# First layer of a four-layer kernel: strips stored in blocks of 16 columns, values formed once per strip, one bias tile for both query halves

## The chip, the cores and the metric

The kernel runs on one core of one Trainium2 chip. The metric is the device time of one execution in microseconds; the median of several runs is compared. A core has five engines with instruction streams of their own, which meet through semaphores: TensorE (PE, whose weight loads are listed apart as PEld), VectorE (DVE), ScalarE (ACT), GpSimd (POOL) and SyncE (SP, which here only starts DMAs). TensorE writes its results to PSUM, and DVE or ACT move them from there to SBUF.

## The reference

The program is a stack of four residual layers on images of shape (2, 128, 128, 128). Only the first is touched: a group norm, and then overlapping window attention. Each window of 16 x 16 pixels asks; its keys and values are the 32 x 32 pixels around it, so neighbouring windows share keys and values. The part of the reference that matters, with WS = 16, HS = 8, NH = 4 heads of 32 channels:

```python
xp = jnp.pad(x, ((0, 0), (HS, HS), (HS, HS), (0, 0)), mode='reflect')
w = xp[:, rows][:, :, :, cols]                      # windows of 32 x 32, step 16
center = w[:, HS:HS + WS, HS:HS + WS].reshape(-1, WS * WS, C)
kv = w.reshape(-1, WSH * WSH, C)
q = (center @ Wq.T + bq) ...                        # 256 queries of a window
k = (kv @ Wk.T + bk) ...; v = (kv @ Wv.T + bv) ...  # 1024 keys and values
attn = jnp.einsum('bhqd,bhkd->bhqk', q, k) * scale
attn = attn + bias[:, start:start + WS * WS, :][None]   # by relative position
out = jnp.einsum('bhqk,bhkd->bhqd', jax.nn.softmax(attn), v)
out = out @ Wp.T + bp
...
x = x + layer0(group_norm(x))
```

The other three layers (a Fourier layer with a feed-forward part, a convolution by FFT, a selective scan) follow one after the other. All arithmetic is in float32.

## The kernel before

`layer0` walks over 2 images x 8 rows x 8 windows, 128 windows. A window has 256 queries, in two halves of 128 (`qt` 0 and 1); one half of one window is a unit, and the loop over `u` has one slot for each unit. Each image is normalised by statistics that are taken beforehand; the normalised, transposed image is kept in **strips** of 16 rows and 144 columns (128 and 8 reflected ones at each side), `xs_[b, k]` of shape [128 channels, 16, 144]. A window uses the strips `wh` and `wh + 1`. Three strips are held at a time.

`strip_load` (L219) loads half a strip, `strip_group` (L230) turns four image rows with four transposes and writes them, scaled and shifted, to the strip with one DVE instruction (L238). `strip_sides` (L242) reflects the sides on POOL. `keys` (L247) forms the keys of a strip in six pieces of 384 columns into `kc`. This work for the strip after next, and the statistics of the next image, are cut into pieces that `background` (L470) puts at the ends of the slots.

For each window, `pixels` (L287) copies its two 16 x 32 patches together on POOL (L294), `queries` (L299) makes `qT` with two matmuls of 128 columns (L305) and one DVE instruction (L311), and `values` (L317) makes the 1024 values in two groups of four matmuls (L323). ACT evicts the first group (L328), DVE the second (L330).

For each unit, `scores` (L332) multiplies queries and keys, 4 heads x 512 keys at a time; `biased` (L348) adds the relative bias and finds the largest score in one DVE instruction for each head (L358); `exponentials` (L364) takes the least of the negated maxima (L368) and runs four ACT instructions over 1024 elements (L370); `turn` (L375) transposes 512 probabilities (L385) and copies them out, on DVE (L388) for the pieces 0, 2, 4 and on ACT (L390) for the pieces 1, 3, 5, 6, 7; `outputs` (L392) multiplies probabilities and values (L401).

For each window, `reciprocals` (L406), `spread` (L419), `weighted` (L431), `project` (L440) and `measure` (L460) divide by the sums, project, add the residual, store, and take statistics for the next layer. `spread` turns the reciprocals with two matmuls against the identity (L423).

The relative bias lies in one tile of 2 halves x 4 heads x 1024, loaded by 32 DMAs on ACT's queue (L179). The PSUM buffers set much of the order: `tps` for transposes has two, `misc` only one, and every piece of keys, queries, values, projection, measurement and background goes through that one. `in_order` (L114) fixes each engine's order as written:

```python
                if first:
                    project(m - 1)
                if second and edge(m + 1):
                    values(m + 1, 0)
                if live:
                    turn(u, 4)
...
                if second:
                    spread(m)
                if ahead:
                    exponentials(u + 1)
                if second and edge(m + 1):
                    values(m + 1, 1)
                if live:
                    outputs(u)
```

`first` is the slot of a window's first half, `second` that of its second half. Between windows of one image `edge` holds; at the change of image the strips and the window's queries and values are made at once instead.

Of the kernel before, what the change touches and what calls it, by code (L numbers as in the profile page):

```python
# [134 lines left out]
def layer0(tc, cs, ins, x, x1, stats1):  # L135
# [3 lines left out]


    nc = tc.nc
    NH, HD, WS, HS = 4, 32, 16, 8
    HP = HW + 2 * HS
    NW = HW // WS
    qscale = HD ** -0.5
    with ExitStack() as ctx:
# [19 lines left out]

        bias = w.tile([P, 2, NH, 1024], F32, name="relbias")
        tab = ins["table_rev"]
        for qt in range(2):
            for h in range(NH):  # L170
                for r in range(4):
                    ry = HS + 4 * qt + r
                    src = bass.AP(
                        tab.tensor,
                        tab.offset + h * tab.shape[1] + 736 - 31 - 47 * ry,
                        [[1, 32], [47, 32], [1, 32]],
                    )
                    p0 = 96 - 32 * r
                    nc.scalar.dma_start(  # L179
                        bias[p0 : p0 + 32, qt, h, :].rearrange("p (a b) -> p a b", b=32), src  # L180
                    )

# [12 lines left out]
        stats, affine = {}, {}  # L195
        xs_, kc = {}, {}

# [21 lines left out]
        def strip_load(b, k, half):  # L219
            r0 = 16 * k - 8 + 8 * half  # L220
            flip = r0 < 0 or r0 >= HW
            if flip:
                r0 = 1 if r0 < 0 else HW - 9
            xl = two.tile([P, 8, C], F32, name=f"xs_{b}_{k}_{half}", tag="xl")
            nc.sync.dma_start(xl, x[b, r0 : r0 + 8].rearrange("r w c -> w r c"))
            if half == 0:
                xs_[b, k] = three.tile([P, WS, HP], F32, name=f"xp_{b}_{k}", tag="xp")
            xs_[b, k, half] = (xl, flip)

        def strip_group(b, k, half, g, ps, tag):  # L230
            xl, flip = xs_[b, k, half]
            sc, sh = affine[b]
            tps = ps.tile([P, 4, P], F32, name=f"xq_{b}_{k}_{half}_{g}", tag=tag)
            for j in range(4):
                r = 4 * g + j
                nc.tensor.transpose(tps[:, j, :], xl[:, 7 - r if flip else r, :], cs.ident)
            r = 8 * half + 4 * g
            nc.vector.tensor_scalar(  # L238
                xs_[b, k][:, r : r + 4, HS : HS + HW], tps, sc, sh, ALU.mult, ALU.add
            )  # L240

        def strip_sides(b, k):  # L242
            xp = xs_[b, k]
            nc.gpsimd.tensor_copy(xp[:, :, 0:HS], xp[:, :, 2 * HS : HS : -1])
            nc.gpsimd.tensor_copy(xp[:, :, HS + HW : HP], xp[:, :, HP - 10 : HP - 18 : -1])

        def keys(b, k, j):  # L247
            if j == 0:
                kc[b, k] = three.tile([P, WS, HP], F32, name=f"kc_{b}_{k}", tag="kc")
            cols = slice(384 * j, 384 * j + 384)  # L250
            kps = ps_m.tile([P, 512], F32, name=f"kps_{b}_{k}_{j}", tag="misc")
            nc.tensor.matmul(
                kps[:, 0:384], wt["k"], xs_[b, k].rearrange("p a b -> p (a b)")[:, cols],
                start=True, stop=True,
            )
            nc.vector.tensor_scalar(
                kc[b, k].rearrange("p a b -> p (a b)")[:, cols], kps[:, 0:384],
                bcol["k"], None, ALU.add,
            )

        def strip_now(b, k):
            for half in range(2):
                strip_load(b, k, half)
                for g in range(2):
                    strip_group(b, k, half, g, ps_t, "tps")
            strip_sides(b, k)
            for j in range(6):
                keys(b, k, j)

        wins = [(b, wh, ww) for b in range(NB) for wh in range(NW) for ww in range(NW)]  # L270
# [15 lines left out]

        def pixels(m):  # L287

            b, wh, ww = wins[m]
            c0 = ww * WS  # L290
            v = held.setdefault(m, {})
            xw = one.tile([P, 2, 512], F32, name=f"xw_{m}", tag="xw")
            for g in range(2):
                nc.gpsimd.tensor_copy(  # L294
                    xw[:, g].rearrange("p (a b) -> p a b", b=32), xs_[b, wh + g][:, :, c0 : c0 + 32]
                )
            v["xw"] = xw

        def queries(m):  # L299
            b, wh, ww = wins[m]  # L300
            c0 = ww * WS
            v = held.setdefault(m, {})
            qps = ps_m.tile([P, 512], F32, name=f"qps_{m}", tag="misc")
            for g in range(2):
                nc.tensor.matmul(  # L305
                    qps[:, P * g : P * g + P], wt["q"],
                    xs_[b, wh + g][:, 8 - 8 * g : 16 - 8 * g, c0 + HS : c0 + HS + WS],
                    start=True, stop=True,
                )
            qT = two.tile([P, 256], F32, name=f"qT_{m}", tag="qT")  # L310
# [5 lines left out]

        def values(m, g):  # L317
            v = held[m]
            if g == 0:
                v["v"] = two.tile([P, 8, P], F32, name=f"v_{m}", tag="v")  # L320
            vps = ps_m.tile([P, 512], F32, name=f"vps_{m}_{g}", tag="misc")
            for j in range(4):
                nc.tensor.matmul(  # L323
                    vps[:, j * P : (j + 1) * P], v["xw"][:, g, j * P : (j + 1) * P], wt["v"],
                    start=True, stop=True,
                )
            if g == 0:
                nc.scalar.copy(v["v"][:, 0:4, :], vps)  # L328
            else:
                nc.vector.tensor_copy(v["v"][:, 4:8, :], vps)  # L330

        def scores(u, g):  # L332

            m, qt = divmod(u, 2)
            b, wh, ww = wins[m]
            c0 = ww * WS
            v = held[m]
            v["sps", qt, g] = []
            for h in range(NH):
                hp = slice(HD * h, HD * h + HD)  # L340
                sps = ps_s.tile([P, 512], F32, name=f"sps_{u}_{g}_{h}", tag=f"sps{h}")
                nc.tensor.matmul(  # L342
                    sps, v["qT"][hp, qt * P : (qt + 1) * P], kc[b, wh + g][hp, :, c0 : c0 + 32],
                    start=True, stop=True,
# [3 lines left out]
        def biased(u, g, h):  # L348
# [3 lines left out]
            if g == 0 and h == 0:  # L352
                v["s", qt] = two.tile([P, NH, 1024], F32, name=f"s_{u}", tag="s")
                v["nm", qt] = two.tile([P, 3, NH], F32, name=f"nm_{u}", tag="nm")
                if qt == 0:
                    v["sums"] = two.tile([P, 2, NH], F32, name=f"sums_{m}", tag="sums")
            cols = slice(512 * g, 512 * g + 512)
            nc.vector.tensor_tensor_reduce(  # L358
                v["s", qt][:, h, cols], v["sps", qt, g][h], bias[:, qt, h, cols],
                op0=ALU.add, op1=ALU.min, scale=-1.0, scalar=3.0e38,  # L360
# [31 lines left out]
        def outputs(u):  # L392
            m, qt = divmod(u, 2)
            v = held[m]
            if qt == 0:
                v["ops"] = ps_o.tile([P, 256], F32, name=f"ops_{m}", tag="ops")
            pT = v["pT", qt]
            for j in range(8):
                for h in range(NH):
                    hp = slice(HD * h, HD * h + HD)  # L400
                    nc.tensor.matmul(  # L401
                        v["ops"][hp, qt * P : (qt + 1) * P], v["v"][:, j, hp], pT[:, h, j, :],
                        start=(j == 0), stop=(j == 7),
# [15 lines left out]
        def spread(m):  # L419
            v = held[m]  # L420
            rps = ps_m.tile([P, 512], F32, name=f"rps_{m}", tag="misc")
            for qt in range(2):
                nc.tensor.matmul(  # L423
                    rps[:, qt * P : (qt + 1) * P], v["recx"][:, qt, :], cs.ident,
                    start=True, stop=True,
                )
# [43 lines left out]
        def background(u):  # L470
# [13 lines left out]
            if b + 1 < NB:  # L484
# [9 lines left out]
                else:  # L494
# [14 lines left out]
                    if 12 <= t <= 14:  # L509
                        keys(b + 1, 0, t - 12)  # L510

        slots = 2 * len(wins)
        with in_order(tc):
# [5 lines left out]
            strip_now(0, 0)  # L519
            strip_now(0, 1)  # L520
            residual(0)
            pixels(0)
            queries(0)
            values(0, 0)
            values(0, 1)
            for u in range(-1, slots + 3):
# [3 lines left out]
                if qt == 1 and ahead and (m + 1) % (NW * NW) == 0 and m >= 0:  # L530

                    b = wins[m + 1][0]
                    for j in (3, 4, 5):
                        keys(b, 0, j)
                    strip_now(b, 1)
                    pixels(m + 1)
                    queries(m + 1)
                    values(m + 1, 0)
                    values(m + 1, 1)
                edge = lambda n: n < len(wins) and n % (NW * NW) != 0  # L540
# [13 lines left out]
                if first:  # L554
                    project(m - 1)
                if second and edge(m + 1):
                    values(m + 1, 0)
                if live:
# [8 lines left out]
                if qt == 0 and 0 <= m < len(wins):  # L567
                    if m + 1 < len(wins):
                        residual(m + 1)
                    if edge(m + 1):  # L570
                        pixels(m + 1)
                        queries(m + 1)
                if second:
                    spread(m)
                if ahead:
                    exponentials(u + 1)
                if second and edge(m + 1):
                    values(m + 1, 1)
                if live:
                    outputs(u)  # L580
                if first:
                    measure(m - 1)
# [1289 lines left out]
```

## Time and profile before

| what | value |
|---|---|
| time, median of 3 runs | 18506.04 us (18495.7 to 18506.94) |
| the profiled execution: its time, its span | 18497.56 us, 18495.8 us |
| first exponential of the first layer (L370) | 119.53 us |
| last reciprocal of the first layer (L410) | 3408.1 us |
| layer 0, strip transposes evicted (L238) | 809 ns each, 72 |
| values on PE (L323) | 2048 records, 304.2 us busy |
| values evicted on ACT (L328), on DVE (L330) | 585 ns and 692 ns each, 128 of each |
| pixel copies on POOL (L294) | 612 ns each, 256 |
| query matmuls (L305) | 512 records, 79.4 us busy |
| reciprocals turned on PE (L423) | 512 records, 78.2 us busy |
| biased scores on DVE (L358) | 683 ns each, 2048 |

A matmul of two float32 operands has two records in the trace, a transpose one. Records on PE overlap, so that busy time is smaller than the number of records times their mean duration. In the timeline a row has the start, the duration, the engine, the line, the operation with what it writes and reads, how many were merged, and in brackets how long the engine stood idle before it and who released it. The whole first layer is about 3,419 us of the span; the remaining layers take the rest.

### The profile page before, as it was taken

The page shows a single profiled execution, that of the slowest core. Times are in us where ns is not written, and L with a number is a line of the kernel's source. Part 1 is how long each engine was busy: PE and PEld are TensorE (multiplying, and loading weights), DVE is VectorE, ACT ScalarE, POOL GpSimd, SP SyncE. Part 2 cuts the span into 40 slices and gives each one's busy share as a digit, 9 for nine tenths or more (in the row PEclk, how much of TensorE's full clock was granted, in tenths as well). Part 3 has the DMA queues.
Part 4 walks back from the last instruction along what each step waited for, and adds up shares of the span by engine and source line. Part 5 has one row for each costly group of instructions (what it writes and reads, how often), then busy time and mean ns, then how long its engine had stood idle before and what let it go on. Part 6 is the DMA issues. An engine that isn't in the chain of part 4 may idle for free. (4 is left out here: it accounts for less than half of the span.)

```text
span 18495.8 us, 280256 instructions
## 1 busy us (share of the span) xinstructions
PE 14497.6 (78%) x98938; PEld 8455.1 (46%) x98938; DVE 15999.1 (87%) x20731; ACT 14932.9 (81%) x30141; POOL 11956.1 (65%) x6710
## 2 busy tenths in 40 slices
PE   7888888887567777777777777777777777777778
PEld 5665666674223344444444444444444444444445
DVE  6666666335888899999999999999999999999996
ACT  4665666333445799999999999999999999999984
POOL 0000000011000399999999999999999999999981
PEclk9999999889779899999999998999999989999999
DMA  2000000121114544444444454544444444455546
GB/s 49 23 23 22 16 16 16 55 72 55 49 48 147 174 119 119 118 126 126 127 114 119 120 128 126 126 118 116 120 126 127 126 122 115 116 122 128 132 129 191
DMA packets 1228553, 1861.32 MB, mean 101 GB/s; under 512 B 120781, under 2 KB 587469, under 8 KB 1224846
## 3 DMA queue, kind: packets, MB, share of 16 engines
q1 hardware_dynamic: 1157374, 1817.40, 37.2%
q10 hardware_dynamic: 69776, 26.00, 0.6%
q8 instruction: 785, 12.86, 0.3%
q14 instruction: 618, 5.06, 0.1%
HBM read 1398.48 MB, written 444.60 MB: 100 GB/s over the span
## 5 line engine op out<-in xcount | busy, mean ns | idle before, releaser
L1599 DVE TENSOR_TENSOR_SCAN hs<-da,states,ups 128x512 f32<-128x512 f32 x8192 | 9920.7, 1262 | 248.9 <-PE ups L1591 235.9
L1617 POOL TENSOR_TENSOR hs<-hs,cb 128x2048 f32<-128x2048 f32 x2048 | 9406.4, 4593 | 310.1 <-POOL but L1554 185.2
L1591 PE MATMUL ups<-ident,but 128*128 128x128 f32 x32768 | 5576.7, 301 | 2578.9 <-DVE hs L1599 1718.8
L1591 PEld LDWEIGHTS ups<-ident,but 128*128 128x128 f32 x32768 | 3873.7, 151 | 6179.9 <-DVE hs L1599 3526.1
L1559 ACT ACTIVATE but<-du,bt 128x256 f32<-128x256 f32 x12800 | 5328.7, 497 | 4.7 <-DVE du L1440 4.2
L1535 ACT ACTIVATE da<-db,na 128x512 f32<-128x512 f32 x8192 | 5224.1, 710 | 19.1 <-DMA db<-dd 17.8
L1573 PE MATMUL yps<-hs,sel 128*32 128x512 f32 x16384 | 2495.2, 685 | 60.7 <-POOL hs L1617 48.2
L1554 POOL TENSOR_TENSOR but<-du,bt 128x256 f32<-128x256 f32 x3584 | 2148.8, 620 | 15.2 <-DVE du L1440 15.2
L282 POOL TENSOR_TENSOR xres<-xres,rowb 128x256 f32<-128x256 f32 x128 | 93.2, 728 | 2641.3 <-DMA xres<-in_x 2512.5
L390 ACT COPY pT<-tps 128x512 f32<-128x512 f32 x1280 | 723.8, 586 | 1123.3 <-PE tps L385 1123.3
L385 PE MATMUL tps<-ident,s 128*128 128x128 f32 x8192 | 1180.8, 283 | 367.5 <-DVE pT L388 273.2
L358 DVE CUSTOM_DVE_ANT_0 s<-sps,relbias 128x512 f32<-128x512 f32 x2048 | 1321.6, 683 | 114.6 <-PE sps L342 109.2
L385 PEld LDWEIGHTS tps<-ident,s 128*128 128x128 f32 x8192 | 889.0, 142 | 898.8 <-issue 486.0
L370 ACT ACTIVATE s<-s,nm 128x1024 f32<-128x1024 f32 x1024 | 1163.5, 1137 | 85.3 <-DVE nm L368 82.1
L1130 POOL MEMSET xpad<- 128x34 f32 x8 | 1.3, 162 | 1242.5 <-PE xs L1021 1178.1
L1611 ACT COPY states<-hs 128x4 f32<-128x4 f32 x2048 | 380.9, 186 | 274.9 <-DVE hs L1599 274.7
L342 PE MATMUL sps<-kc,qT 32*128 32x512 f32 x4096 | 596.7, 650 | 0.8 <-DVE nm L358 0.8
L388 DVE COPY pT<-tps 128x512 f32<-128x512 f32 x768 | 526.6, 686 | 55.0 <-PE tps L385 54.5
L1573 PEld LDWEIGHTS yps<-hs,sel 128*32 128x32 f32 x16384 | 340.7, 114 | 486.0 <-issue 309.6
L1323 PE MATMUL xdps<-xc,xpw 128*40 128x512 f32 x1024 | 541.4, 611 | 12.3 <-POOL xd L1260 12.3
L1355 PE MATMUL dtps<-xd,dtw 65*128 65x512 f32 x1024 | 535.6, 605 | 0.0
L725 POOL TENSOR_TENSOR xr<-xr,row_ln_b 128x512 f32<-128x512 f32 x64 | 81.2, 1270 | 701.5 <-ACT acc L687 353.5
(286 smaller groups left out, 16784.7 us busy)
## 6 DMA issues: line engine op xcount, KB each, us to landing
db<-dd SPq DMA_DIRECT2D x1024, 512.0 KB
cb<-cd SPq DMA_DIRECT2D x1024, 256.0 KB
xc<-xs SPq DMA_DIRECT2D x256, 512.0 KB
dd<-dl SPq DMA_DIRECT2D x256, 512.0 KB
ut<-xst SPq DMA_DIRECT2D x128, 512.0 KB
yc<-ysb SPq DMA_DIRECT2D x128, 512.0 KB
yf<-yc SPq DMA_DIRECT2D x128, 512.0 KB
ys<-yt SPq DMA_DIRECT2D x128, 512.0 KB
```

Source lines behind the costliest of these rows:

```text
L342: nc.tensor.matmul(sps, v["qT"][hp, qt * P : (qt + 1) * P], kc[b, wh + g][hp, :, c0 : c0 + 32], start=True, stop=True,)
L358: nc.vector.tensor_tensor_reduce(v["s", qt][:, h, cols], v["sps", qt, g][h], bias[:, qt, h, cols], op0=ALU.add, op1=ALU.min, scale=-1.0, s ...
L370: nc.scalar.activation(s[:, h, :], s[:, h, :], AF.Exp, bias=nm[:, 2, h : h + 1], scale=-1.0, accum_out=v["sums"][:, qt, h : h + 1],)
L385: nc.tensor.transpose(tps[:, j, :], v["s", qt][:, h, k0 : k0 + P], cs.ident)
L390: nc.scalar.copy(dst, tps)
L1535: nc.scalar.activation(da[:, j, :], held[i]["db"][:, 4 * e + j, :], AF.Exp, scale=na[:, k, c : c + 1])
L1554: nc.gpsimd.tensor_tensor(but[:, j, :, n, :], du[:, tb], bt[:, tb, c : c + 1].unsqueeze(2).to_broadcast([P, 8, 32]), ALU.mult,)
L1559: nc.scalar.activation(but[:, j, :, n, :], du[:, tb], AF.Copy, scale=bt[:, tb, c : c + 1])
L1573: nc.tensor.matmul(v["yps"][e][32 * j : 32 * j + 32, :], sel, hs[:, j, :], start=(q == 0), stop=(q == 3),)
L1591: nc.tensor.transpose(ups[:, tb * P : (tb + 1) * P], v[("but", q, tb // 2)][:, tb % 2, 4 * e + j].rearrange("p n c -> p (n c)"), cs.ident,)
L1599: nc.vector.tensor_tensor_scan(o, a, u, state[:, c0 + j : c0 + j + 1], ALU.mult, ALU.add)
L1617: nc.gpsimd.tensor_tensor(hs, hs, v["cb"][:, s // 2, :].unsqueeze(1).to_broadcast([P, 4, T]), ALU.mult)
```

## The change

- A strip is stored as 9 blocks of 16 rows x 16 columns instead of 16 rows of 144 columns. A window's patch of a strip is then two whole blocks, without a gap between them. `strip_group` writes each piece with two DVE instructions of 256 elements, since every 16 columns of the image fall into two blocks; `strip_sides` has four smaller POOL copies for two. The keys of a strip get the same layout.
- The values are formed for a whole strip, 18 matmuls in five groups, and held in `vs`; `outputs` reads them from there. `row_values` makes the groups of the strip after next in the second slots of the windows 3 to 7 of a row (counted from 0), at the place where the first group of the window's values stood. Those of the first two strips of an image are made before the loop, or at the change of image (three groups before the strip is made, five after `outputs`). `pixels` is gone.
- `queries` has four matmuls of 64 columns for two of 128, since the 16 columns in the middle lie in two blocks.
- The bias is one tile of 36 rows for each head and block column; the two halves of the queries read it 4 rows apart. There are 32 DMAs as before, with runs of 16 elements for 32. `biased` reads its bias operand as two runs of 256.
- `spread` uses a transpose for each half instead of a matmul.

```diff
-        bias = w.tile([P, 2, NH, 1024], F32, name="relbias")
+        BR = 36
+        bias = w.tile([P, NH, 2, BR, WS], F32, name="relbias")
...
+                        [[1, 32], [47, BR], [1, WS]],
...
+                    nc.scalar.dma_start(bias[p0 : p0 + 32, h, a], src)
...
-            nc.vector.tensor_scalar(
-                xs_[b, k][:, r : r + 4, HS : HS + HW], tps, sc, sh, ALU.mult, ALU.add
-            )
+            for n in range(2):
+                src = tps.rearrange("p r (c n w) -> p c r n w", n=2, w=HS)[:, :, :, n]
+                dst = xs_[b, k][:, n : n + NW, r : r + 4, HS * (1 - n) : HS * (2 - n)]
+                nc.vector.tensor_scalar(dst, src, sc, sh, ALU.mult, ALU.add)
...
+        def values(b, k, j):
+            if j == 0:
+                vs[b, k] = three.tile([P, 2 * NC, P], F32, name=f"v_{b}_{k}", tag="v")
+            n0, n1 = 4 * j, min(4 * j + 4, 2 * NC)
+            xp = xs_[b, k].rearrange("p a r c -> p (a r c)")
+            vps = ps_m.tile([P, 512], F32, name=f"vps_{b}_{k}_{j}", tag="misc")
+            for n in range(n0, n1):
+                nc.tensor.matmul(
+                    vps[:, (n - n0) * P : (n - n0 + 1) * P], xp[:, n * P : (n + 1) * P], wt["v"],
+                    start=True, stop=True,
+                )
+            (nc.scalar.copy if j % 2 else nc.vector.tensor_copy)(
+                vs[b, k][:, n0:n1, :].rearrange("p n c -> p (n c)"), vps[:, 0 : (n1 - n0) * P]
+            )
...
+            halves = qps[:, 0:256].rearrange("p (g r n c) -> p g n r c", g=2, r=HS, n=2)
             for g in range(2):
...
+                for n in range(2):
+                    nc.tensor.matmul(
+                        halves[:, g, n], wt["q"],
+                        xs_[b, wh + g][
+                            :, ww + n, 8 - 8 * g : 16 - 8 * g, HS * (1 - n) : HS * (2 - n)
+                        ],
+                        start=True, stop=True,
+                    )
...
-            cols = slice(512 * g, 512 * g + 512)
+            blocks = lambda a: a.rearrange("p (a n) -> p a n", a=2)
+            r0 = 4 * (1 - qt) + WS * g
...
+                bias[:, h, :, r0 : r0 + WS, :].rearrange("p a r c -> p a (r c)"),
...
-                nc.tensor.matmul(
-                    rps[:, qt * P : (qt + 1) * P], v["recx"][:, qt, :], cs.ident,
-                    start=True, stop=True,
+                nc.tensor.transpose(
+                    rps[:, qt * P : (qt + 1) * P], v["recx"][:, qt, :], cs.ident
                 )
...
+        def row_values(m):
+            b, wh, ww = wins[m]
+            k = wh + 2
+            if k <= NW and ww >= 3:
+                values(b, k, ww - 3)
+            if k > NW and b + 1 < NB and ww >= 6:
+                values(b + 1, 0, ww - 6)
...
+            for k in range(2):
+                for j in range(5):
+                    values(0, k, j)
             residual(0)
-            pixels(0)
             queries(0)
-            values(0, 0)
-            values(0, 1)
...
+                    for j in (2, 3, 4):
+                        values(b, 0, j)
                     strip_now(b, 1)
-                    pixels(m + 1)
                     queries(m + 1)
-                    values(m + 1, 0)
-                    values(m + 1, 1)
...
-                if second and edge(m + 1):
-                    values(m + 1, 0)
+                if second:
+                    row_values(m)
...
-                if second and edge(m + 1):
-                    values(m + 1, 1)
                 if live:
                     outputs(u)
+                if second and m + 1 < len(wins) and not edge(m + 1):
+                    for j in range(5):
+                        values(wins[m + 1][0], 1, j)
```

## The prediction

> **What bounds it now.** I took the page's slices first, then groups of instructions, waits by engine and the timeline inside the first layer. The change touches only this layer, which ends at 3,419 us of 18,495.8; from there on I expect the same time. In the windows view no engine of the layer is full:
>
> ```profile
> 130.00:1740.00 1610.00, 1379.07 (x16390) 994.85 (x16382) 1103.13 (x3010) 995.46 (x1767) 151.79 (x330) 0.99 0.08 22
> ```
>
> (columns: PE, PEld, DVE, ACT, POOL busy us, PE clock, DMA share, GB/s). PE is 86% busy, DVE 69%, ACT 62%. So a loop of waits sets the pace, and deleted PE time counts only where PE is in that loop. One window's two slots, timeline:
>
> ```profile
> 2009.60 1.15 ACT L370 ACTIVATE s<-s,nm 128x1024 f32<-128x1024 f32 x1
> 2009.63 1.16 PE L323 MATMUL vps<-wvT,xw 128*128 128x128 f32 x8 [0.50 <-ACT rT L428]
> 2010.72 1.95 PE L401 MATMUL ops<-pT,v 128*32 128x128 f32 x64
> 2012.61 0.65 PE L236 MATMUL xq<-ident,xs 128*128 128x128 f32 x4
> ...
> 2014.03 0.41 DVE L434 TENSOR_TENSOR aT<-ops,rT 128x256 f32<-128x256 f32 x1
> ...
> 2014.36 0.68 DVE L358 CUSTOM_DVE_ANT_0 s<-sps,relbias 128x512 f32<-128x512 f32 x1
> ...
> 2022.38 1.15 ACT L370 ACTIVATE s<-s,nm 128x1024 f32<-128x1024 f32 x1 [0.57 <-DVE nm L368]
> ```
>
> Call the first exponential of a window's first unit E1 (2009.60), of its second unit E2 (2022.38), of the next window E1'. From E1 the chain is PE: second values group, outputs, a background transpose; then DVE. The exponentials themselves are over at E1 + 4.65, before DVE starts the next biased scores at E1 + 4.76. So E1 to E2 is bound by **PE's queue**. From E2 on, DVE's reciprocal waits for ACT's last exponential (27.12), then DVE runs nearly gapless to E1' (34.94 in the next period): ACT and DVE bind, PE does not.
>
> **1. The values.** Read off the exponentials' starts, E1 to E2 is 12.19 us without background work ahead of it, 12.77 with a strip transpose, 13.03 with keys; E2 to E1' is 12.57 in nearly all windows. What remains of E1 to E2 when a window has no values group is in this trace, once, at the change of image:
>
> ```profile
> 1780.18 1.96 PE L401 MATMUL ops<-pT,v 128*32 128x128 f32 x64
> ...
> 1780.68 1.15 ACT L370 ACTIVATE s<-s,nm 128x1024 f32<-128x1024 f32 x1
> ...
> 1785.22 0.56 ACT L390 COPY pT<-tps 128x512 f32<-128x512 f32 x1
> ...
> 1787.17 0.66 PE L385 MATMUL tps<-ident,s 128*128 128x128 f32 x4 [0.23 <-ACT pT L390]
> ...
> 1788.92 0.69 DVE L358 CUSTOM_DVE_ANT_0 s<-sps,relbias 128x512 f32<-128x512 f32 x1 [0.36 <-PE sps L342]
> ...
> 1790.66 0.61 PE L305 MATMUL qps<-xp,wqT 128*128 128x128 f32 x4
> ...
> 1791.37 0.48 DVE L311 TENSOR_SCALAR qT<-qps,bqcol 128x256 f32<-128x256 f32 x1
> 1792.01 1.15 ACT L370 ACTIVATE s<-s,nm 128x1024 f32<-128x1024 f32 x1 [0.57 <-DVE nm L368]
> ```
>
> Outputs start before the exponentials, and E1 to E2 is 11.33. Late next is **ACT**: its copy of turn 1 (85.22) queues behind four exponentials, then come turn 3, its copy, turn 4 (87.17), scores. I take 11.33 for every kind of window. The background work then fits under ACT: with a strip transpose DVE would reach the second group of biased scores at about E1 + 7.8, with keys about the same, and PE's scores allow it at E1 + 8.24.
>
> The first values group (L323 after turn 3) saves nothing: turn 4 behind it waits for a copy that ends at the same moment (04.98 against 05.09). The new strip groups sit in that place in five windows of eight. With an odd j ACT evicts, as now; with an even one DVE gets a copy (L330, 0.69) before turn 4's, where it now idles 0.15 and then 0.36 for scores: at most 0.2, taken as 0. If that cover were gone, three groups in eight windows at 0.69 would cost 33 us over 128 windows. The 149 us of pixel copies on POOL and the freed ACT and DVE copies are off the chain.
>
> **2. The queries.** Four matmuls of 64 columns in place of two of 128: eight records instead of four. Four take about 0.44 us (L305: 77.5 us busy over 126 windows, 0.61 with the pipeline's tail). No N=64 row exists; the nearest is layer 1's N=48:
>
> ```profile
> 3440.00:3494.00 54.00, 53.99 (x254) 54.00 (x254) 13.63 (x15) 0.50 0.55 167
> ```
>
> (that tile alone: PE, PEld, ACT): 54.0/254 = 0.213 us per record at clock 0.50, so 0.106 at full clock, with PEld as full as PE. A record of half the width is as dear, since it reloads the weights. Against it, the table in the Trainium skill's "TensorE: Matmul & The Clock Gate", section "Back-to-back issue gap", gives up to 64 columns about 60 cycles and 128 columns 134: by that the split is free. The row decides: +0.43. Behind it wait qT, the maximum and E2; PE's results now come 0.10 before DVE is ready (91.27 against 91.37), so 0.43 − 0.10 = **+0.33**, after which E1 to E2 is 11.66. Bounds 0 and 0.43.
>
> **3. Blocks, bias, reciprocals.** L358 keeps 512 elements; its bias operand becomes two runs of 256. Nearest rows: L434, two reversed runs, 416 ns, against L451, 419 ns, plain. I take 0, bounds −10 and +50 ns. Strip evictions: two of 256 (L311: 481 ns) for one of 809, +0.15, under ACT's cover in the loop; exposed in all 72 groups, 11 us. POOL's side copies: four for two, smaller, about +0.4 us a strip, exposed only where strips are made at once. The 32 bias loads have 36,864 runs of 64 bytes for 32,768 of 128, on ACT's queue: ACT's first instruction is at 96.3, PE first needs ACT near 109; covered unless they take over 12 us more. Single-pass reciprocals take 0.22 off 0.49 of PE, but ACT's rT copy follows turn 7's copy anyway: 0.
>
> **4. Start and change of image.** Ten values groups stand before the first window instead of two. PE is at half clock there; groups then follow every 2.8 us (107.00 to 109.81), half groups about 1.6: 8 × 2.8 + 2 × 1.6 = 25.6 against 4.8 now, +21; with sides, evictions and queries **+23**. At the image change: three groups more ahead of the strip (+4.6), two fewer after (−4.8), queries and strip +1.4, and five groups after outputs, two of them evicted behind four exponentials, which push E2 back by about 7: **+8**.
>
> **Sum.** The new period is 11.66 + 12.57 = 24.23. Rows of eight windows without clock stalls are now 202.9 us (first image), 201.75 (second), 198.1 (last row, no background); all become 193.8. Gain: 8 × 9.1 + 7 × 7.9 + 4.3 = 132. Less 23 and 8: 101.
>
> **The clock speaks against it.** Stretches of 3.41 us (PE etc., clock):
>
> ```profile
> 3227.48:3230.89 3.41, 0.75 (x7) 0.69 (x7) 2.17 (x7) 1.60 (x4) 0.53 (x2) 1.00 0.01 2
> 3230.89:3234.31 3.42, 3.42 (x20) 3.09 (x22) 1.78 (x6) 1.17 (x2) 0.00 (x0) 0.50 0.02 5
> ```
>
> After a stretch with PE 22% busy, the next runs at half clock; the window takes 26.35 instead of 24.76: 1.6 us. Going through the layer from 130 us on that grid, 26 drops follow: every full-clock stretch under 42% is followed by one, and of those above 44% all but one kept the clock; half clock ends after a stretch over about 80%. The skill (same page, "Part 1: The HAM clock gate") asks for about one whole idle window, and its section "Why this matters for your kernels" warns of idle gaps above about 3 us. Longest gap in the loop: 2.9 us, before and after, so its rule predicts no drop. By the trace, work removed after turn 3 lengthens the light stretch: in a slot without background about 80% of phases are light instead of 60%, and slots with a strip transpose but no values become so in about 15%. I estimate some 32 spells, some longer: **−13** of gain.
>
> Net −88: 18,497.56 of the profiled run becomes about 18,410; on the median of 18,506.04, 8.5 above it, **18,418**.
>
> **Rivals.** A difference under 0.2% (37 us) can't be told from none.
> - *The split queries are free* (skill's table): 127 × 0.33 = 42 more gain, **18,376**. Against it: the N=48 row. Chance 0.12.
> - *Slower: the clock gate.* The period of 24.23 is near seven stretches (23.9), so a bad phase can persist through many windows, and with the values gone PE may also miss the 80% that end a spell. At 1.6 us a drop it turns the 88 into a loss from 55 further spells; in nearly every window (100 further) it gives **18,578**. For it: the last row, which drops every second window. Against: most slots keep background or values work. Chance 0.15.
> - *Gain eaten*: the two-run bias read costs 40 ns on 16 operations a window (127 × 0.64 = 81), **18,499**. Against: L434. Chance 0.15, with dearer strip evictions, a spell in two windows of five, or a longer start.
> - Forecast: 0.58, own range 18,370 to 18,460.
>
> Range 18,345 to 18,530: its ends take in free queries with fewer drops, and half of the clock's loss. Faster 0.68 (forecast, free queries, less the forecast's weak end), same 0.15, slower 0.17.
>
> **What would show it.** E1 to E2 near 11.66 in every kind of window and E2 to E1' still 12.57; qT waiting about 0.3 us for PE; L358 at 683 ns; the first exponential near 142 instead of 119.5; the half-clock stretches counted. Wrong if L358 grows, if E1 to E2 stays above 12, or if half clock takes over whole rows.

## The result, and the profile after

The changed kernel took **18,421.01 us**, the median of four runs (18,414.82 to 18,430.42), against 18,504.73 for the kernel before (18,495.7 to 18,506.94, four runs): a ratio of 0.9958, 95% interval 0.9946 to 0.997, or 84 us less. Forecast were 18,418 us, 88 less.

The profiled execution of the changed kernel took 18,430.42 us (span 18,428.6), at the upper end of its runs. Between the two profiles:

| us | before | after | difference |
|---|---|---|---|
| first exponential of layer 1 | 119.5 | 144.9 | +25.4 |
| from there to the last reciprocal | 3288.6 | 3191.6 | −97.0 |
| rest of the span | 15,087.6 | 15,092.1 | +4.5 |

So the layer ends 71.6 us earlier, and the remaining layers stay as they were. First the timeline of one window of the changed kernel, to be laid beside the two of the prediction:

```profile
612.15 1.96 PE L404 MATMUL ops<-pT,v 128*32 128x128 f32 x64
...
612.92 1.15 ACT L371 ACTIVATE s<-s,nm 128x1024 f32<-128x1024 f32 x1
...
617.47 0.56 ACT L391 COPY pT<-tps 128x512 f32<-128x512 f32 x1
...
619.41 0.66 PE L386 MATMUL tps<-ident,s 128*128 128x128 f32 x4 [0.23 <-ACT pT L391]
...
621.16 0.69 DVE L358 CUSTOM_DVE_ANT_1 s<-sps,relbias 128x512 f32<-128x512 f32 x1 [0.36 <-PE sps L341]
...
622.89 1.00 PE L318 MATMUL qps<-xp,wqT 128*128 128x64 f32 x8
...
623.94 0.48 DVE L326 TENSOR_SCALAR qT<-qps,bqcol 128x256 f32<-128x256 f32 x1 [0.25 <-PE qps L318]
...
624.59 1.15 ACT L371 ACTIVATE s<-s,nm 128x1024 f32<-128x1024 f32 x1 [0.91 <-DVE nm L369]
...
637.15 1.15 ACT L371 ACTIVATE s<-s,nm 128x1024 f32<-128x1024 f32 x1
```

E1 is 612.92, E2 624.59, E1' 637.15: 11.67 and 12.56. The outputs now start before E1, no values group follows them, and the second biased scores come 8.24 after E1, released by PE's scores. In this order PE is led by ACT: its copy of turn 1 (617.47) starts when the fourth exponential is over. New is the wait of qT for the split queries, 0.25. Groups of instructions over the layer, first two of the kernel before, then those of the changed one (busy us, mean ns of one; idle us before them with releasers):

```profile
L305 PEld LDWEIGHTS qps<-xp,wqT 128*128 128x128 f32 x512 | 68.1, 194 | 3.7 <-DVE kc L256 3.7
L311 DVE TENSOR_SCALAR qT<-qps,bqcol 128x256 f32<-128x256 f32 x128 | 61.5, 481 | 2.6 <-PE qps L305 2.6
```

```profile
L358 DVE CUSTOM_DVE_ANT_1 s<-sps,relbias 128x512 f32<-128x512 f32 x2048 | 1321.6, 683 | 138.9 <-PE sps L341 133.6 <-PE tps L386 0.2
L318 PE MATMUL qps<-xp,wqT 128*128 128x64 f32 x1024 | 130.4, 271 | 1.2 <-DVE kc L264 0.7 <-DVE v L290 0.5
L318 PEld LDWEIGHTS qps<-xp,wqT 128*128 128x128 f32 x1024 | 126.0, 194 | 2.7 <-DVE kc L264 1.9 <-DVE v L290 0.8
L246 DVE TENSOR_SCALAR xp<-xq,sc,sh 128x256 f32<-128x256 f32 x144 | 71.0, 540 | 87.2 <-PE xq L239 87.1
L326 DVE TENSOR_SCALAR qT<-qps,bqcol 128x256 f32<-128x256 f32 x128 | 61.9, 484 | 35.2 <-PE qps L318 35.2
```

The biased scores take 683 ns as before, so the two-run bias read costs nothing. The queries' 1024 records, half as wide, take 130.4 us where 512 took 79.4; their weight loads are twice as many and take 126.0 us where they took 68.1. qT waits 35.2 us in all for them, where it waited 2.6.

PE, PEld, DVE, ACT and POOL busy, PE clock, DMA share and GB/s of 1500 us in the first image (the kernel before has PE 1285.22, DVE 1029.26, ACT 925.12, POOL 143.68, clock 0.99 in the same stretch):

```profile
150.00:1650.00 1500.00, 1280.34 (x15222) 891.38 (x15222) 1049.74 (x2902) 926.17 (x1659) 82.40 (x212) 0.98 0.08 23
```

No engine is full here either. POOL lost its copies and nothing came of it, as expected; PE does less work for a window and is as busy: in the same 1500 us 61 windows begin instead of 59, and more of the time is at half clock (64 us against 24). The spells at half clock begin as before, with a light stretch; here one in the second image (columns as above):

```profile
2166.34:2169.75 3.41, 1.29 (x12) 0.86 (x8) 1.05 (x4) 2.73 (x5) 0.52 (x2) 1.00 0.00 0
2169.75:2173.16 3.41, 2.27 (x10) 1.90 (x11) 2.84 (x8) 0.58 (x1) 0.00 (x0) 0.50 0.01 2
2173.16:2176.58 3.42, 3.42 (x15) 1.59 (x14) 1.29 (x2) 0.00 (x0) 0.00 (x0) 0.50 0.00 0
```

PE is 38% busy at full clock, and then runs at half clock for **two** stretches of 3.41 us, 66% and 100% busy. Before, each spell but that of the image change was over after one. Between the first exponential and the last reciprocal 24 spells begin in the kernel before, 99 us at half clock; in the changed one 34 begin, 14 of them with two stretches, 181 us in all.

### The profile page after: what moved, and what is told of

Its sections match the earlier page's. It is cut to its first block, busy times and chain, and to the rows that moved or that the text cites. A ratio compares the mean times of both kernels' runs of the same rounds, so it can differ in the third digit from the quotient of the medians.

```text
span 18428.6 us, 277686 instructions
## 1 busy us (share of the span) xinstructions
PE 14403.4 (78%) x97794; PEld 8312.0 (45%) x97794; DVE 15967.4 (87%) x20729; ACT 14862.3 (81%) x30049; POOL 11820.0 (64%) x6490
## 5 line engine op out<-in xcount | busy, mean ns | idle before, releaser
L386 PE MATMUL tps<-ident,s 128*128 128x128 f32 x8192 | 1228.9, 287 | 433.5 <-DVE pT L389 269.3
L358 DVE CUSTOM_DVE_ANT_1 s<-sps,relbias 128x512 f32<-128x512 f32 x2048 | 1321.6, 683 | 138.9 <-PE sps L341 133.6
```

Source lines behind the costliest of these rows:

```text
L358: nc.vector.tensor_tensor_reduce(blocks(v["s", qt][:, h, 512 * g : 512 * g + 512]), blocks(v["sps", qt, g][h]), bias[:, h, :, r0 : r0 + WS ...
L386: nc.tensor.transpose(tps[:, j, :], v["s", qt][:, h, k0 : k0 + P], cs.ident)
```

## The experiments

The kernel before was run beside each group of experiments: median 18,486.03 (7 runs) with the first four, 18,501.76 (13 runs) with the next four, 18,504.7 (7 runs) with the last three. Where a kernel has one run, its difference holds to about the scatter of these, up to 28 us either way; its trace decides then.

**Which values group was on the chain.** Two kernels leave out half of the values each: one group is made for a window and used for both strips. x1_no_second, an edit of the kernel before (x2_no_first leaves out the other group in the same way):

```diff
-                if second and edge(m + 1):
-                    values(m + 1, 1)
...
-    v["ops"][hp, qt * P : (qt + 1) * P], v["v"][:, j, hp], pT[:, h, j, :],
+    v["ops"][hp, qt * P : (qt + 1) * P], v["v"][:, j % 4, hp], pT[:, h, j, :],
```

> The kernel before, with the second values group of every window (the one between ACT's copy of the turned reciprocals and the outputs) left out; the outputs use the first group for both strips, so half of the values is not computed. Theory (PE's queue binds E1 to E2, ACT is the floor behind it): E1 to E2 becomes 11.33 us in every kind of window (12.2 to 13.0 before), E2 to E1' stays 12.57; about 180 us less, near 18,325. Rival (PE's load as such sets the time): the same gain as from leaving out the first group, about 127 x 1.1 = 140 us, near 18,365.

It took 18,316.9 us (one run), 169 less. Timeline of the same window:

```profile
619.46 1.95 PE L401 MATMUL ops<-pT,v 128*32 128x128 f32 x64
...
620.00 1.15 ACT L370 ACTIVATE s<-s,nm 128x1024 f32<-128x1024 f32 x1
...
631.37 1.15 ACT L370 ACTIVATE s<-s,nm 128x1024 f32<-128x1024 f32 x1 [0.57 <-DVE nm L368]
```

E1 to E2 is 11.33 in windows without keys and 11.36 with them (here 11.37), where it was 12.2 to 13.0; E2 to E1' stays at 12.57. With the group gone the outputs start before E1: the bound by PE's queue is confirmed, and with it the 11.33 taken from a single place at the change of image. (The group's DVE copy goes with it; that the matmuls were the binding part is read off PE's order, not tried apart.)

> The kernel before, with the first values group of every window (the one after turn 3) left out; the outputs use the second group for both strips. Theory: E1 to E2 and E2 to E1' stay as before (12.2 to 13.0 and 12.57), since turn 4 waits for a copy that ends at the same moment; only start and image change gain about 6 us, and more stretches fall under 42% PE, so that half-clock spells grow from 25 to over 30: between 18,480 and 18,530. Rival (PE's load): about 140 us less, near 18,365.

It took 18,583.27 us (one run): **97 us more for less work**, and 53 above the end of the expected range. Undisturbed windows are exactly those of the kernel before (24.75 to 25.6, E2 to E1' 12.57): leaving out the first group shortens none of them, as the prediction said. But 75 spells begin in the loop, where 24 did, and the half clock grows from 99 to 352 us. In the windows view, two stretches in a row:

```profile
2193.71:2197.12 3.41, 1.36 (x11) 1.16 (x12) 3.41 (x10) 0.80 (x2) 0.53 (x2) 1.00 0.00 0
2197.12:2200.54 3.42, 3.42 (x16) 1.59 (x15) 1.75 (x6) 0.00 (x0) 0.00 (x0) 0.50 0.00 0
```

While DVE is busy throughout, PE has 40% to do, and it pays in the next stretch. The group off the chain had kept the clock up. This is the slower rival of the prediction, in another kernel: its mechanism is real. The loop grew by 3389.3 − 3288.6 = 100.7 us, 2.0 for each of the 51 further spells: a window with a spell of one stretch is 1.4 to 1.6 us longer, with two stretches 2.4 to 2.7.

**Are split queries free?** One matmul for each strip half again: the strip gets a block of padding, so that the two half blocks in the middle can be addressed with one stride. x3_one_query, an edit of the changed kernel:

```diff
-                for n in range(2):
-                    nc.tensor.matmul(
-                        halves[:, g, n], wt["q"],
-                        xs_[b, wh + g][
-                            :, ww + n, 8 - 8 * g : 16 - 8 * g, HS * (1 - n) : HS * (2 - n)
-                        ],
-                        start=True, stop=True,
-                    )
+                c0 = 256 * ww + 16 * (8 - 8 * g) + HS
+                mid = xs_[b, wh + g].rearrange("p a r c -> p (a r c)")[:, c0 : c0 + 496]
+                mid = mid.rearrange("p (n x) -> p n x", n=2)[:, :, 0:P]
+                nc.tensor.matmul(
+                    halves[:, g], wt["q"],
+                    mid.rearrange("p n (r c) -> p n r c", c=WS)[:, :, :, 0:HS],
+                    start=True, stop=True,
+                )
```

> The changed kernel, with the queries of each strip half in one matmul of 128 columns again (two runs of 8 columns per row, read 248 elements apart, in the block layout). Theory (a matmul of 64 columns is as dear as one of 128): E1 to E2 falls from 11.66 to 11.33, the wait of qT for PE goes, period 23.90; 127 x 0.33 = 42 us less than the changed kernel, near 18,380. The period is then exactly seven clock stretches (23.9), so spells may settle in one phase: 18,360 to 18,420. Rival (the split is free, by the isolated gap): E1 to E2 stays 11.66, no change, 18,421.

18,353.45 us (18,349.88 to 18,363.64), ratio 0.9926 [0.9909, 0.9942]. Its timeline:

```profile
612.40 1.15 ACT L371 ACTIVATE s<-s,nm 128x1024 f32<-128x1024 f32 x1
...
622.37 0.61 PE L320 MATMUL qps<-xp,wqT 128*128 128x128 f32 x4
...
623.73 1.15 ACT L371 ACTIVATE s<-s,nm 128x1024 f32<-128x1024 f32 x1 [0.57 <-DVE nm L369]
```

E1 to E2 is 11.33, qT waits for nothing, and the loop took 3149.4 us against 3191.6: 42.2 less, where 127 × 0.33 makes 42. So the split cost what the N=48 row said, and the rival of free queries falls. (The median fell by 68 us, more than the loop. The run's first exponential came at 126.5 instead of 144.9, because here the values groups of the start fell in a stretch at full clock, every 1.9 us instead of 2.85. How long the start takes depends on the clock, which this experiment didn't set.)

**What the clock costs.** Idle transposes of the identity, eight between turn 1 and turn 2 of every second slot and six after turn 3 where no values are made, fill PE in the light stretch. Their result is read by nobody. x4_filler, an edit of the changed kernel (x8_before_filler has the eight alone, in the kernel before):

```diff
+        def filler(u, c, n):
+            fps = ps_m.tile([P, 512], F32, name=f"fill_{u}_{c}", tag="misc")
+            for j in range(n):
+                nc.tensor.transpose(fps[:, (j % 4) * P : (j % 4 + 1) * P], cs.ident, cs.ident)
...
                     if live:
                         turn(u, i)
+                    if second and i == 1:
+                        filler(u, 0, 8)
...
                 if second:
                     row_values(m)
+                    if not made(m):
+                        filler(u, 1, 6)
```

> The changed kernel, with idle transposes of the identity added on PE in every second slot: 8 between turn 1 and turn 2, and 6 after turn 3 where no values are made. Nothing reads them. Theory (half clock follows a stretch of 3.41 us with PE under 42% busy, not a long gap): spells in the loop fall from 35 to under 10, E1 to E2 and E2 to E1' keep 11.66 and 12.57; some 27 x 1.6 = 43 us less than the changed kernel, near 18,378. Rival (gaps over 3 us decide, or the spells cost nothing): no gain, 18,421 or more, since 127 x 14 transposes are added.

18,361.4 us (18,348.95 to 18,370.46), ratio 0.993 [0.9915, 0.9945]. Spells go from 34 to 2, both at the change of image, all but a few windows take 24.22 or 24.23, and the loop 3135.2 us instead of 3191.6. In the same 1500 us as above PE has more to do and the clock is full:

```profile
150.00:1650.00 1500.00, 1344.91 (x16117) 961.66 (x16116) 1067.75 (x2951) 942.93 (x1687) 84.39 (x219) 1.00 0.08 23
```

The loop is 56.4 us shorter. Laid beside this kernel window by window, the changed one is longer in 30 windows, each with a spell, by 54.1 us in all (start and image change left out): **1.8 us a spell**, 1.4 for most of those with one stretch, 2.2 to 2.5 for those with two.

> The kernel before, with eight idle transposes of the identity between turn 1 and turn 2 of every second slot. Theory (the share of busy PE in a stretch decides the clock): the 23 spells in the loop nearly vanish, the windows keep 24.8 to 25.6 us, and the time falls by 23 x 1.6 = 37 us although PE does more. Rival (PE's load costs time): 127 x 8 x 0.11 = 112 us more.

18,478.46 us (18,464.53 to 18,495.36, 10 runs), ratio 0.9987 [0.9978, 0.9996]; spells 24 to 3, undisturbed windows unchanged, loop 3258.8 instead of 3288.6, that is 29.8 us less. Its first window, the image change and one window ahead of it have half clock of their own and take 5.8 us more than in the kernel before. In the other windows that kernel is longer in 22, each with a spell, by 35.7 us: **1.6 us a spell**. In these windows the change thus brought 54.1 − 35.7 = 18.4 us of further spells.

**Whether start and image change can be had back.** Only the first group of each of an image's two strips is made ahead of its first window (two of the first strip in the second image), the others in the second slots of its windows 0 to 4. x5_late, an edit of the changed kernel:

```diff
             for k in range(2):
-                for j in range(5):
-                    values(0, k, j)
+                values(0, k, 0)
...
+            if wh == 0:
+                for kk, j in ((0, 1), (1, 1)) if ww == 0 else ((0, 2), (1, 2)) if ww == 1 \
+                        else ((0, 3), (1, 3)) if ww == 2 else ((ww - 3, 4),) if ww < 5 else ():
+                    if b == 0 or (kk, j) != (0, 1):
+                        values(b, kk, j)
```

> The changed kernel, with only one values group for each of the two first strips ahead of the first window and at the image change; the other groups are made in the second slots of the first row, two in each of the windows 0 to 2, one more in the windows 3 and 4. Theory (the start pays 2.8 us for each group at half clock): the first exponential comes 20 us earlier, near 125; the two windows at the image change lose some 10 us; the slots with two groups pay up to 1.5 us each: about 22 us less than the changed kernel. Rival (the start waits for something else, such as the bias loads): the first exponential stays later than 140 and nothing is gained.

18,393.54 us (one run). The first exponential came 20.5 earlier and the two windows of the image change took 12.1 less, but the windows 1 to 4 of each image take 26.06 to 26.37 instead of 24.23, with E2 to E1' 14.4 to 14.6 instead of 12.57, and the very first one 30.4 instead of 26.9. The layer ends only 11.5 us earlier: a miss by half. Two values groups in one slot are on the chain again.

**Is ACT really what is late next?** The DVE takes turn 1, so that no copy queues behind the exponentials there. x6_turn1, an edit of the changed kernel:

```diff
-            if g == 0 and h < 3:
+            if c in ((0, 1, 4) if qt == 0 else (0, 2, 4)):
```

> The changed kernel, with the copy of turn 1 on DVE and that of turn 2 on ACT in the first slots. Theory (after the values are gone, E1 to E2 waits for ACT's copy of turn 1, which queues behind four exponentials): E1 to E2 falls from 11.66 to about 11.0, E2 to E1' stays 12.57; some 85 us less than the changed kernel if the clock spells stay as they are. Rival (DVE or PE is already as late as ACT): E1 to E2 stays at 11.6 or more, no gain.

18,423.8 us (one run), no gain. Timeline of a window without background work:

```profile
612.01 1.15 ACT L371 ACTIVATE s<-s,nm 128x1024 f32<-128x1024 f32 x1
...
616.10 0.68 DVE L389 COPY pT<-tps 128x512 f32<-128x512 f32 x1
...
623.23 1.15 ACT L371 ACTIVATE s<-s,nm 128x1024 f32<-128x1024 f32 x1 [0.90 <-DVE nm L369]
```

11.22 instead of 11.66: there ACT's copy was the bound. With background work E1 to E2 is mostly 11.7 to 12.0, above the 11.66 it had: DVE, which evicts that work, now also has the copy, and in the next window, with keys, runs without a gap from their eviction (637.86) to 642.64. The mean is 11.7. So in the changed kernel DVE lies close behind ACT; that the background work fits beneath it, as forecast, was right, with little to spare.

**Reciprocals in two passes** (the matmul against the identity of the kernel before, in `spread` of the changed kernel).

> The changed kernel with the reciprocals turned by two-pass matmuls again. Theory (ACT's copy of them stands behind turn 7's copy in any case): E1 to E2 11.66 and E2 to E1' 12.57 as in the changed kernel, time within 15 us of it. Rival (the pass is on the chain): E2 to E1' grows by 0.2 us, some 25 us more.

18,439.79 us (one run), 19 more. E2 to E1' stays at 12.57, undisturbed windows take 24.23, or 24.27 with keys: at most 0.04 of the two passes is on the chain, and the rival of 0.2 falls. The layer ends 12.5 us later, and 42 spells begin in its loop where 34 did. Beside x4_filler its windows are 68.1 us longer, those of the changed kernel 54.1: the difference is that of the spells. Why they became more stays open.

**Better than both.** One query matmul, fillers, late values, in two forms; x10_spread puts the late groups one to a slot, on DVE, where x9_best has two in a slot. (x7_all also had the turn of x6_turn1.)

> The changed kernel with all four edits: one query matmul for each strip half, the idle transposes in the second slots, late values groups in the first row, turn 1 copied by DVE in the first slots. If each acts on its own place: E1 to E2 about 10.7, E2 to E1' 12.57, no spells in the loop, first exponential near 125: about 185 us less than the changed kernel, ratio to the kernel before near 0.986. If turn 1 brings nothing, about 110 us less.

> The changed kernel with three edits: one query matmul for each strip half, the idle transposes in the second slots, late values groups in the first row; the copies of turn 1 and 2 as in the changed kernel. With turn 1 on DVE the windows with background work took 24.2 us and the bare ones 23.4; without it all should take 11.33 + 12.57 = 23.9. No spells in the loop, first exponential near 123, the first row of each image some 11 us longer: about 115 us less than the changed kernel, ratio to the kernel before near 0.990.

> The same, with the late groups spread over the slots of the first row: one in each first slot (after the outputs, evicted by DVE) and one in each second slot, none doubled. If it is the second group of a slot that costs (it waits for the only misc buffer of PSUM), the first row of each image is 5 to 10 us shorter than with doubled groups, everything else the same: some 15 us less. Rival (any added group costs, wherever it stands): no gain.

| kernel | median us (lowest to highest) | ratio to before, 95% |
|---|---|---|
| x7_all | 18,334.95 (18,326.38 to 18,346.87) | 0.9912 [0.9896, 0.9929] |
| x9_best | 18,323.06 (18,314.86 to 18,330.81) | 0.99 [0.9885, 0.9914] |
| x10_spread | 18,319.8 (18,307.07 to 18,324.73) | 0.9896 [0.988, 0.9913] |

In x9_best nearly every window takes 23.89 (11.33 + 12.56), the windows 1 to 4 of an image 25.7 to 26.0. In x10_spread those take 24.6 to 25.1, and its layer ends 6.7 us earlier, not 15; so a single added group costs too, only less than two in one slot, and the times of the two kernels can't be told apart. Both take about 100 us less than the changed kernel; their layers end 116 and 123 us earlier than its layer, some 98 of them by the queries (42) and the clock (56), if the two add up as in the runs apart. The turn of x6_turn1 adds nothing that the times show: x7_all took 86 us less than the changed kernel, where 110 were expected without a gain by the turn (its layer ends 112 earlier; undisturbed windows 23.44 to 24.2).

## Why the prediction was right

**1, the values: right in place and size.** E1 to E2 is 11.66 in all eight kinds of window and E2 to E1' 12.56 to 12.57: the period of 24.23 is the one forecast. That PE's queue was the bound (x1_no_second), that the first group saved nothing (x2_no_first), and that ACT is late next (x6_turn1, bare windows) each has a run. In the two kernels with fillers, rows without a spell take 202.9 us in the first image and 201.7 in the second, after the change 193.8: the gains of 9.1 and 7.9 a row that the forecast's 132 us are made of.

**2, the queries: right.** The row of the trace (0.106 us for a record of 48 columns) was right against the gap table: eight records of 64 columns took 1.00 us with the pipeline's tail, four of 128 took 0.61, so 0.098 for each further record. x3_one_query has the 42 us back. The table's own section in the Trainium skill ("TensorE: Matmul & The Clock Gate", section "Back-to-back issue gap") says that it holds for an isolated matmul and counts too little at small N, because the weight load is not in it; so the prediction read more into it than it states. From the formula of the same page's section "LDWEIGHTS (loading the stationary operand)", columns / 1.2, an estimate for 128 columns is 107 ns, near the 98 measured at full clock; at half clock the N=48 row has 213, which the formula doesn't give. That the weight loads set the pace is read off their 126.0 us in 130.4, not tried apart.

**3, blocks, bias, reciprocals: right at nothing.** L358 683 ns in both; a strip group's two evictions take 0.99 us for 0.81; the bias loads ended sooner, not later (below).

**4, start and image change: +30 and +11.6 us for +23 and +8.** The first exponential came 25.4 later, and the first window, 26.91 us for 22.97, lost 3.9 where the forecast has it gain 1.1: half clock of the start reached into it (to 152.5, before to 124.8), and a spell followed at 162.7. The two windows of the image change took 88.5 us against 78.6, where the sum counts them as 1.6 shorter. Both terms were too small; how long the start takes hangs on where the clock rises, as x3_one_query showed.

**The clock: right in kind, short in size.** The price of a spell before the change was right, 1.6 us (35.7 / 22). Forecast were some 32 spells for 26 over the layer, some of them longer, and 13 us; in the loop 34 begin for 24, and they cost 18.4 us more. What was sized too small is the second condition, the end of a spell: 14 of the 34 lasted two stretches, six of these after a first one with PE at 80.2%, where the lightest stretch that ended one had 83%. The prediction named this in its slower rival.

The sum in the traces, gain positive: 132 for the windows without spells, less 30 for the start with its first window, 12 for the image change and 18 for the spells, makes 72; the layer ends 71.6 us earlier. Forecast were 132 − 23 − 8 − 13 = 88. So the gain was right, and each of the three losses too small, by 7, 4 and 5. That the medians differ by 84 and meet the forecast within 3 us is partly luck: the profiled execution of the changed kernel was its slowest, and the rest of its span 4.5 us longer. Of the rivals, free queries fell (x3_one_query), the eaten gain fell (L358 683 ns), and the clock gate took 18 us instead of turning the sign.

One detail stays open: turn 4 waits for ACT's copy of turn 3 (619.41, after a copy of 618.77), though `tps` has two buffers and DVE's copy of turn 2 had ended. It was not tried apart.

## What to carry to other kernels

Find the start-to-start times of one repeated instruction that every loop contains, and look for a place in the trace where the suspected work happens to be missing: here one window at the change of image gave the 11.33 us that x1_no_second and x3_one_query then had in all windows. Work that an engine does off the chain isn't always worthless on TensorE: before taking it away, count the PE share of the stretches in which the clock is decided. Here the same amount of work left out in two places gave 169 us less (x1_no_second) and 97 more (x2_no_first), and idle transposes took 56 us off the loop (x4_filler). A matmul that is cut in two along its moving columns loads its weights twice: 42 us here.

## What the runs showed of the hardware

- The granted clock follows PE's busy share over stretches of 3.41 us. In the kernel before, outside the image change, every full-clock stretch up to 40.8% was followed by half clock and those from 44.3% kept it. Over all kernels the border is not sharp: in x1_no_second a stretch of 42.9% was dropped and one of 41.1% kept, in x2_no_first some up to 46.8% were dropped and from 47.7% all kept, and in the changed kernel one of 58% was dropped. Half clock went on after every stretch under 79%; above that it ended after most and went on after some. The Trainium skill (same page, "Part 1: The HAM clock gate") asks for a whole idle window; the longest gap on PE in the loop was 2.9 us before and 2.8 after, and spells came all the same.
- Transposes of the identity count as activity: 14 or 8 of them in a window end nearly all spells (34 to 2 in x4_filler, 24 to 3 in x8_before_filler).
- Spells come back with the rows of eight windows. In the changed kernel one begins in the first window of every row, and in the last row, which makes no values, in each of the first seven. That its period of 24.23 us, close to seven stretches (23.9), holds a bad phase is not shown: x3_one_query, with 23.90, has 33 spells for 34.
- The bias loads on ACT's queue, before and after (start, duration):

```profile
0.72 95.58 ACTq L179 DMA_DIRECT2D relbias<-in_table_rev  x32
```

```profile
0.72 79.43 ACTq L184 DMA_DIRECT2D relbias<-in_table_rev  x32
```

More and shorter runs ended 16 us sooner: 36,864 packets of 64 bytes at 11.2 ns (mean) against 32,768 of 128 bytes at 15.7. The same difference stands in other profiles (76.9 and 78.4 us for the whole of it in x4_filler and x9_best, 96.7 in x8_before_filler). The prediction had allowed for the opposite.
